# One gather in forty-six moved from GpSimd to row-by-row transfers issued by SyncE, in a three-layer graph network

## The chip, the cores and the metric

The kernel runs on one core of a Trainium2 chip. The metric is the device time of one execution in microseconds. Engines are called PE (TensorE), DVE (VectorE), ACT (ScalarE), POOL (GpSimd) and SP (SyncE); SP computes nothing here and only issues transfers, as POOL does with its gathers.

## The reference

6250 nodes with 256 features each, 100,000 edges sorted by destination, three edge types, three layers:

```
ew = edge_attr @ edge_w + edge_b                    # 100000 x 256, once
for l in range(3):
    msg = relu(x[src] * ew)                         # gather of 100000 rows
    out = x @ roots[l] + biases[l]
    for i in range(3):
        h = segment_sum(msg * (edge_type == i), dst) / max(count_i, 1)
        out = out + h @ weights[l, i]
    x = x + relu(out)
result = layernorm(x0 + x)
```

The 100,000 sources are random nodes, so `x[src]` is a fetch of 100,000 separate rows of 1 KB from the chip's main memory, in every layer.

## The kernel before, in words

Edges are cut into tiles of 128; two tiles are a pair, two pairs (four tiles) share one buffer `xs` of 128 partitions x 2 x 2 x 256 numbers. There are 391 pairs, 782 tiles a layer. A layer is one loop over steps `it`, written out by hand; each engine runs the instructions in the order in which the loop issues them. One step takes in one pair:

- `gather(pair(9))` (line 989, in `gather_pair`): POOL issues two indirect transfers, one a tile; each reads 128 indices of `src_io` from the chip's own memory and fetches 128 rows. There are `ROWS` = 8 buffers `xs`, so POOL may be up to eight buffers ahead of their readers.
- SP loads `at`, the edges' attributes of eight pairs (line 570, three buffers), for `pair(9)`; `make_ew` uses it at `pair(5)`, four steps later (line 624, PE, after ACT's seed on line 611).
- `weigh(pair(3))`: DVE multiplies (line 646) and ACT applies relu (line 648), over a whole buffer of two pairs. `one_hot` (line 654) makes 0/1 matrices from destinations, and `reduce(pair(0))` (lines 668 and 676, PE) sums messages by node with them. `add` (line 704, DVE) adds the sums into `acc` at a place held in registers, which line 697 loads eight at a time.
- A block of 128 nodes whose edges are done is multiplied by the weights (line 732), finished by DVE (lines 763 and 766) and, in layers 0 and 1, written by SP to the table `x_mid` (line 768) that the next layer gathers from. In the last layer SP loads `x0` (line 792) and stores the output (line 785) instead.

The first six pairs of a layer need nothing from node block 0 (it is added later) and are gathered before the layer begins. All other gathers of the layer wait until the whole of `x_mid` is written. Every transfer of SP and ACT is given one of eight completion semaphores in turn, and before a semaphore is used again the issuing engine waits until the transfer that used it before has landed.

Of the kernel before, what the change touches and what calls it, by code (L numbers as in the profile page):

```python
# [8 lines left out]
F32 = mybir.dt.float32  # L9
BF = mybir.dt.bfloat16  # L10
I32 = mybir.dt.int32
# [431 lines left out]
def ordered_path(ctx, tc, x, attr_laid, A, weights, roots, biases, edge_w, edge_b, out, src, src_i, seg, place_i, consts, x_root,  # L443
# [6 lines left out]
    nc = tc.nc  # L450
    P = 128
    N, D = x.shape
    E = src.shape[0]
# [4 lines left out]
    U = T // 2  # L458
# [4 lines left out]
    order, _, moved, least, most = schedule(N, E, 1)  # L463
# [16 lines left out]
    big = ctx.enter_context(tc.tile_pool(name="big", bufs=1))  # L480
# [51 lines left out]
    rows = ctx.enter_context(tc.tile_pool(name="rows", bufs=ROWS))  # L532
# [6 lines left out]
    def first_of(p, n):  # L539
        return p == 0 or order[p - 1] // n != order[p] // n  # L540

    def last_of(p, n):
        return p == U - 1 or order[p + 1] // n != order[p] // n

    def opens(u):
        p = order.index(u)
        return p == 0 or span_of[order[p - 1]] != span_of[u]
# [20 lines left out]
    def load_at(g):  # L568
        at = edge.tile([P, GROUP // 2, P], F32, name="at", bufs=3)
        nc.sync.dma_start(at.rearrange("p q e -> p (q e)"), attr_laid[g])  # L570
        return at
# [8 lines left out]
    def layer(l, r_sb, b_sb, ats, early, pools):  # L580
# [5 lines left out]
        x_rows = x if l == 0 else x_mid[l - 1]  # L586
        w_sb = wpool.tile([P, R * DC, D], F32, name="w_sb")
        CH = DC + 1 if l == 0 else DC
        xs, ew_ps, ohs, h_ps, h_ss, o_ps, rs = {}, {}, {}, {}, {}, {}, {}
        x0s, mvs, oh_bs, t_ss, places = {}, {}, {}, {}, []  # L590
        r_next, ats_next, early_next = (None, None), {}, {}
        seen = [0]

        def gather(u):
            p = order.index(u)
            if p < FIRST:
                xs[u // 2] = early[u // 2]
            else:
                if first_of(p, 2):
                    xs[u // 2] = room(rows, D)  # L600
                gather_pair(nc, xs[u // 2], x_rows, src_i, u)

        def pairs_of(q):
            return range(min(2, U - 2 * q))
# [23 lines left out]
        def gather_early(p):  # L628
            u = order[p]
            if first_of(p, 2):  # L630
                early_next[u // 2] = room(rows, D)
            gather_pair(nc, early_next[u // 2], x_mid[l], src_i, u)
# [172 lines left out]
        for it in range(-11, max(starts) + 7):  # L805
            def pair(k):
                return order[it + k] if 0 <= it + k < U else None
            if pair(AHEAD) is not None:
                gather(pair(AHEAD))
            if l < L - 1 and 0 <= it + AHEAD - U < FIRST:  # L810
                gather_early(it + AHEAD - U)
            if l == 0 and it == 20:
                find_came()
            if pair(AHEAD) is not None and pair(AHEAD) // GROUP not in ats:
                ats[pair(AHEAD) // GROUP] = load_at(pair(AHEAD) // GROUP)
            if l == 0 and it >= -4 and (it + 4) % 20 == 0 and (it + 4) // 20 * 6 < NT - 1:
                load_x((it + 4) // 20 * 6)
            if it == 10:
                nc.sync.dma_start(w_sb, weights[l].rearrange("r (c p) e -> p (r c) e", p=P))
            if l == L - 1 and it + 2 in root_at:  # L820
                load_x0(root_at[it + 2])
            if l < L - 1 and it == U - 10:
                r_next = load_root(l + 1)
            if l < L - 1 and U - 10 <= it < U - 8:
                ats_next[at_groups[it - U + 10]] = load_at(at_groups[it - U + 10])

            if pair(0) is not None:
                reduce(pair(0))
            if pair(-1) is not None and closes(pair(-1)) and turned(span_of[pair(-1)]):
                take(span_of[pair(-1)])  # L830
            if pair(5) is not None and first_of(it + 5, 2):
                make_ew(pair(5) // 2)
            for lag in (LAG + 1, LAG):
                if pair(-lag) is not None and closes(pair(-lag)) and turned(span_of[pair(-lag)]) == (lag > LAG):
                    add(span_of[pair(-lag)])
            if pair(-1) is not None and closes(pair(-1)) and turned(span_of[pair(-1)]):
                turn(span_of[pair(-1)])
            if pair(3) is not None and first_of(it + 3, 2):
                if l > 0 and it + 3 < FIRST:
                    complete(pair(3) // 2)  # L840
                if pair(3) // 2 != order[-1] // 2:
                    weigh(pair(3) // 2)

            if pair(3) is not None and pair(3) // 2 == order[-1] // 2:
                weigh(pair(3) // 2, range(pair(3) % 2, pair(3) % 2 + 1))
            if pair(6) is not None and first_of(it + 6, 2):
                seed_ew(pair(6) // 2)
            if it in root_at:
                root_turn(root_at[it])
            if it - 1 in root_at:  # L850
                root_turned(root_at[it - 1])
            if it - 2 in root_at:
                root_mul(root_at[it - 2])
            if it - 3 in root_at:
                root_keep(root_at[it - 3])
            if it == moved:
                move()
            if it - 2 == moved:
                clear(P)
            if it + 1 in node_at and slot_of(node_at[it + 1]) == 0:  # L860
                wrap()
            if it in node_at:
                node_mul(node_at[it], 0)
            if it - 1 in node_at:
                node_end(node_at[it - 1], 0)
            if it - 2 in node_at:
                node_mul(node_at[it - 2], 1)
            if it - 3 in node_at:
                node_end(node_at[it - 3], 1)
                clear(slot_of(node_at[it - 3]))  # L870
            if it - 4 in node_at and l == L - 1:
                deviate(node_at[it - 4])
            if it - 5 in node_at and l == L - 1:
                norm(node_at[it - 5])
            if pair(2) is not None and first_of(it + 2, 2):
                one_hot(pair(2) // 2)
# [21 lines left out]
FIRST = 6  # L898

ASTRAY = 1024  # L900


def spans_of(N, E):
# [31 lines left out]
def schedule(N, E, lag):  # L935

    P = 128
    U = -(-E // (2 * P))
    NT = -(-N // P)
    done = []
    for c in range(NT):
        edges = E * min(1.0, (P * (c + 1) / N) ** 0.5)
        done.append(U if c == NT - 1 else min(U, -(-int(edges) // (2 * P)) + 4))
    K = first_pairs(N, E)
    spans = spans_of(N, E)
    for c in range(NT):  # L950
        span = next(s for s in spans if s[1] >= done[c])
        done[c] = span[1] + turned(span)
    order = list(range(K, U)) + list(range(K - 1, -1, -1))
    moved = done[1] - K + lag
    starts = [0] * NT
    step = moved
    for c in range(2, NT):
        step = starts[c] = max(done[c] - K + lag + 1, step + 4)

    whole = U - int(0.55 * K)  # L960
    starts[1] = max(whole + lag, step + 4)
    starts[0] = max(U + lag - 1, starts[1] + 4)

    node = lambda e: int(N * min(1.0, max(0.0, e / E)) ** 2)
    least = [node(2 * P * u - ASTRAY) for u in range(U)]
    most = [node(2 * P * u + ASTRAY) for u in range(U)]


    for u, v in spans:
        p = max(order.index(u), order.index(v - 1)) + lag + turned((u, v))  # L970
        if u >= K:
            assert all(p <= starts[c] or least[u] >= P * (c + 1) for c in range(2, NT))
            assert p <= moved or least[u] >= 2 * P
            assert all(p < starts[c] or least[u] >= P * c for c in range(8, NT, 8))
            for b in range(RING // P + 1, (most[u] + WIN - 1) // P + 1):
                assert (moved + 2 if b - RING // P == 1 else starts[b - RING // P] + 3) < p
        else:
            assert most[u] <= 2 * P and (p <= starts[1] or most[u] + WIN <= P)
    return order, starts, moved, least, most


def room(rows, D):

    return rows.tile([128, 2, 2, D], F32, name="xs", bufs=ROWS)


def gather_pair(nc, xs, x_rows, src_i, u):
    for i in range(2):
        nc.gpsimd.indirect_dma_start(  # L989
            out=xs[:, u % 2, i, :], out_offset=None, in_=x_rows[:, :],  # L990
            in_offset=bass.IndirectOffsetOnAxis(ap=src_i[:, 2 * u + i:2 * u + i + 1], axis=0))
# [3 lines left out]
def kernel(ctx, tc, x, src, dst, edge_attr, edge_type, weights, roots, biases, edge_w,  # L995
# [32 lines left out]
    with tc.tile_pool(name="look", bufs=1) as look, tc.tile_pool(name="look_p", bufs=2, space=PSUM) as look_p, \  # L1028
# [7 lines left out]
        limits = look.tile([1, 2, U], F32, name="limits")  # L1036
        nc.gpsimd.iota(limits, pattern=[[2 * ASTRAY, 2], [2 * P, U]], base=-ASTRAY, channel_multiplier=0,
                       allow_small_or_imprecise_dtypes=True)
# [120 lines left out]
```

## Time and profile before

| | |
|---|---|
| time, median of 3 runs | 2981.86 us (2981.05 to 2984.7) |
| profiled execution: its time / its span | 2986.33 us / 2984.5 us |
| POOL busy | 2239.8 us in 2355 instructions |
| PE busy | 2656.7 us |
| DVE busy | 1935.5 us |
| ACT busy | 1561.9 us |
| mean granted TensorE clock | 0.97 |
| mean DMA rate | 130 GB/s |

A busy share says how much of the span an engine's instructions took, not whether it set the pace. [...] An operation that is marked "q", as in SPq, is the engine's queue: issuing transfers, loading registers, waiting for semaphores.

### The profile page before, as it was taken

The page shows a single profiled execution, that of the slowest core. Times are in us where ns is not written, and L with a number is a line of the kernel's source. Part 1 is how long each engine was busy: PE and PEld are TensorE (multiplying, and loading weights), DVE is VectorE, ACT ScalarE, POOL GpSimd, SP SyncE. Part 2 cuts the span into 40 slices and gives each one's busy share as a digit, 9 for nine tenths or more (in the row PEclk, how much of TensorE's full clock was granted, in tenths as well). Part 3 has the DMA queues.
Part 4 walks back from the last instruction along what each step waited for, and adds up shares of the span by engine and source line. Part 5 has one row for each costly group of instructions (what it writes and reads, how often), then busy time and mean ns, then how long its engine had stood idle before and what let it go on. Part 6 is the DMA issues. An engine that isn't in the chain of part 4 may idle for free.

```text
span 2984.5 us, 45518 instructions
## 1 busy us (share of the span) xinstructions
PE 2656.7 (89%) x13712; PEld 1836.6 (62%) x13712; DVE 1935.5 (65%) x5485; ACT 1561.9 (52%) x2487; POOL 2239.8 (75%) x2355
## 2 busy tenths in 40 slices
PE   5999999999998888998899889778899889889887
PEld 2666677776765555556676666455555666666655
DVE  6666677777764455566666676445566677777754
ACT  4666666666665445554444444435555544444453
POOL 7777777777777777777777777777777777777775
PEclk9999999999999999999999999899999999999998
DMA  5544444444444434444444444434444444444443
GB/s 163 149 144 136 143 128 128 129 126 130 128 135 127 122 112 125 122 120 128 128 128 125 130 131 133 127 113 143 132 137 133 134 133 136 131 129 131 128 124 95
DMA packets 173574, 387.52 MB, mean 130 GB/s; under 512 B 43450, under 2 KB 78924, under 8 KB 173324
## 3 DMA queue, kind: packets, MB, share of 16 engines
q0 software_dynamic: 112608, 307.65, 36.0%
q1 hardware_dynamic: 53136, 68.50, 7.3%
q10 hardware_dynamic: 7580, 8.37, 0.9%
q8 instruction: 117, 1.92, 0.3%
q14 instruction: 133, 1.09, 0.1%
HBM read 364.88 MB, written 19.46 MB: 129 GB/s over the span
## 4 chain that ended last, share of the span: by engine, by line
PE 40%; POOL 16%; DMA 15%; issue 13%; DVE 7%; ACT 6%; DVEq 1%; ACTq 0%; POOLq 0%
POOL xs L989 16%; DMA xs<-x_mid,src_io 12%; PE ew_p L624 11%; PE h_p L668 9%; PE h_p L676 7%; PE o_p L732 6%; PE r_p L717 4%; DVE xs L646 3%; DMA xs<-in_x_dram,src_io 3%; ACT ew_p L611 2%; ACT xs L648 2%; PE h_p L688 1%; DVE x_root L763 1%; DVE acc L704 1%; PE r_p L709 1%
## 5 line engine op out<-in xcount | busy, mean ns | idle before, releaser
L989 POOL DMA_INDIRECT xs<-x_mid,src_io x1564 | 1490.6, 953 | 485.5 <-issue 373.0
L648 ACT ACTIVATE xs<-xs 128x1024 f32<-128x1024 f32 (+1 forms) x588 | 617.8, 1051 | 1241.4 <-DVE xs L646 1233.3
L646 DVE TENSOR_TENSOR xs<-ew_p,xs 128x512 f32<-128x512 f32 x1167 | 777.2, 684 | 643.9 <-DMA xs<-x_mid,src_io 489.8
L989 POOL DMA_INDIRECT xs<-in_x_dram,src_io x770 | 734.4, 954 | 234.7 <-issue 185.9
L624 PE MATMUL ew_p<-ew_sb,at 64*128 64x512 f32 x2346 | 761.6, 657 | 108.4 <-ACT ew_p L611 102.6
L676 PEld LDWEIGHTS h_p<-oh,xs 128*128 128x128 f32 x5160 | 657.9, 197 | 233.9 <-DVE acc L704 106.3
L676 PE MATMUL h_p<-oh,xs 128*128 128x120 f32 x5160 | 717.0, 287 | 64.8 <-DVE acc L704 59.2
L611 ACT ACTIVATE ew_p<-seed 128x512 f32<-128x512 f32 x1161 | 639.9, 583 | 0.0
L668 PE MATMUL h_p<-xs,oh 128*120 128x256 f32 x2088 | 554.5, 397 | 24.1 <-DVE acc L704 24.0
L654 DVE TENSOR_SCALAR oh<-iota_w,seg_o 128x120 f32<-128x120 f32 x2346 | 517.1, 298 | 0.0
L732 PE MATMUL o_p<-w_sb,acc 128*128 128x256 f32 (+1 forms) x1716 | 445.4, 396 | 29.6 <-DVE x_root L763 14.9
L704 DVE TENSOR_TENSOR acc<-h_p,acc 128x240 f32 (+1 forms) x732 | 323.6, 442 | 180.7 <-PE o_p L732 42.4
L668 PEld LDWEIGHTS h_p<-xs,oh 128*120 128x120 f32 x2088 | 356.6, 187 | 123.3 <-DVE acc L704 34.4
L732 PEld LDWEIGHTS o_p<-w_sb,acc 128*128 128x128 f32 (+1 forms) x1716 | 310.9, 192 | 161.8 <-issue 38.5
L624 PEld LDWEIGHTS ew_p<-ew_sb,at 64*128 64x128 f32 x2346 | 230.0, 188 | 262.1 <-ACT ew_p L611 184.4
L763 DVE SCALAR_TENSOR_TENSOR x_root<-o_p,inv,x_root 128x256 f32<-128x256 f32 (+1 forms) x429 | 205.9, 480 | 59.1 <-PE o_p L732 51.7
L717 PE MATMUL r_p<-r_sb,t_s 128*128 128x256 f32 x588 | 171.4, 417 | 31.6 <-ACT t_s L713 31.6
L658 ACT ACTIVATE oh_b<-oh 128x480 bf16<-128x480 f32 x196 | 116.7, 596 | 102.2 <-DVE oh L654 101.6
L717 PEld LDWEIGHTS r_p<-r_sb,t_s 128*128 128x128 f32 x588 | 106.7, 202 | 83.5 <-ACT t_s L713 47.2
L749 ACT ACTIVATE acc<-zero_o 128x768 f32<-128x768 f32 (+1 forms) x150 | 140.1, 934 | 21.5 <-PE r_p L732 16.4
L688 PEld LDWEIGHTS h_p<-ident_o,h_s 120*128 120x128 f32 x342 | 35.7, 144 | 145.9 <-ACT h_s L684 81.9
L720 DVE TENSOR_TENSOR x_root<-r_p,b_sb 128x256 f32<-128x256 f32 x147 | 61.6, 419 | 64.4 <-PE r_p L717 38.8
(103 smaller groups left out, 898.8 us busy)
## 6 DMA issues: line engine op xcount, KB each, us to landing
at<-in_attr_laid_dram SPq DMA_DIRECT2D x147, 256.0 KB
xs<-x_mid,src_io POOLq DMA_INDIRECT x1564, 2.8
xs<-in_x_dram,src_io POOLq DMA_INDIRECT x770, 2.8
x_mid<-x_all SPq DMA_DIRECT2D x96, 128.0 KB
x_all<-in_x_dram ACTq DMA_DIRECT2D x8, 768.0 KB
x<-in_x_dram SPq DMA_DIRECT2D x48, 128.0 KB
out_dram<-x_all SPq DMA_DIRECT2D x48, 128.0 KB
w_sb<-in_L_gnn_weights_dram SPq DMA_DIRECT2D x3, 768.0 KB
```

What stands on the lines that cost most here:

```text
L611: nc.scalar.activation(ew_ps[u], seed, AF.Copy)
L624: nc.tensor.matmul(ew_ps[2 * q + k].rearrange("p i d -> p (i d)"), at[half, :], ew_sb[half].rearrange("p i d -> p (i d)"), start=False, st ...
L646: nc.vector.tensor_mul(xs[q][:, k], ew_ps[2 * q + k], xs[q][:, k])
L648: nc.scalar.activation(there, there, AF.Relu)
L654: nc.vector.tensor_scalar(ohs[q][:, t, :], iota_w, seg[:, 4 * q + t:4 * q + t + 1], None, op0=ALU.is_equal)
L668: nc.tensor.matmul(by_node[:WK, :D], ohs[u // 2][:, t, :], xs[u // 2][:, u % 2, i, :], start=(i == 0 and opens(u)), stop=(i == 1 and close ...
L676: nc.tensor.matmul(h_ps[span][:, d, :], xs[u // 2][:, u % 2, i, d * P:(d + 1) * P] if d < DC else full_ones, (ohs if d < DC else oh_bs)[u ...
L704: nc.vector.tensor_tensor(there, h_ps[span][:, :CH].rearrange("p c (r w) -> p c r w", r=R), there, op=ALU.add)
L717: nc.tensor.matmul(rs[c][:, 1, :], t_ss[c][:, d, :], r_sb[:, d, :], start=(d == 0), stop=(d == DC - 1))
L732: nc.tensor.matmul(o_p[:n, j, :], acc[:, d, r, slot:slot + n], w_sb[:, r * DC + d, :], start=(d == 0), stop=(d == DC - 1))
L763: nc.vector.scalar_tensor_tensor(root, o_p[:n, j, :], inv[:n, c, r:r + 1], root, op0=ALU.mult, op1=ALU.add)
L989: nc.gpsimd.indirect_dma_start(out=xs[:, u % 2, i, :], out_offset=None, in_=x_rows[:, :], in_offset=bass.IndirectOffsetOnAxis(ap=src_i[:, ...
```

## The change

In each layer 17 of the 782 tiles are no longer gathered by POOL. SP fetches their rows one by one: a list of the sources, `src_s`, lies in the chip's memory; for every eight rows SP loads eight of its numbers into registers, and each row is a transfer of its own, of 1 KB, whose source address comes from a register. The 128 rows of such a tile are issued six in a step (`SINGLES`), from step 0 on, at a place in the loop after `gather` and before the load of `at`, so 17 tiles take 363 steps of some 410. The tile is the second one of the second pair that is in its buffer, and its position lies at least six steps behind the step in which its last row is issued. `weigh`, which reads it, comes three steps before that position. These buffers are a kind of their own, `xs_s`, of which there are two; the other three tiles in them are gathered as before. The same 17 positions are used in all three layers: 28, 48, 70 and so on about every 21 steps up to 369.

```diff
+    per = -(-U * 2 // P)
+    src_s = big.tile([P, per * P], I32, name="src_s")
+    whole = E // (per * P)
+    nc.scalar.dma_start(src_s[:whole, :], src[:whole * per * P].rearrange("(a e) -> a e", e=per * P))
+    singles = []
+    for p in range(U - 12):
+        first = SINGLE_FROM + (len(singles) + 1) * P // SINGLES + 6
+        if p >= first and first_of(p, 2) and order[p] // 2 == order[p + 1] // 2 and order[p] < (whole * per) // 2 - 2:
+            singles.append((order[p + 1], 1))
+    single_of = {u // 2: (u, i) for u, i in singles}
...
-                if first_of(p, 2):
+                if first_of(p, 2) and u // 2 not in single_of:
                     xs[u // 2] = room(rows, D)
-                gather_pair(nc, xs[u // 2], x_rows, src_i, u)
+                gather_pair(nc, xs[u // 2], x_rows, src_i, u, [i for i in range(2) if (u, i) not in singles])
...
+        def fetch(n):
+
+            for r in range(n, n + SINGLES):
+                if r // P >= len(singles):
+                    return
+                u, i = singles[r // P]
+                if r % P == 0:
+                    xs[u // 2] = rows.tile([P, 2, 2, D], F32, name="xs_s", bufs=2)
+                t = 2 * u + i
+                if r % LOADED == 0:
+                    _, loaded = nc.values_load_multi_w_load_instructions(
+                        src_s[t // per:t // per + 1, t % per * P + r % P:t % per * P + r % P + LOADED],
+                        engines=[mybir.EngineType.SP], min_val=0, max_val=N - 1,
+                        skip_runtime_bounds_check_because="it is the number of a node")
+                    sources[:] = loaded
+                nc.sync.dma_start(xs[u // 2][r % P:r % P + 1, u % 2, i, :], x_rows[bass.ds(sources[r % LOADED], 1), :])
...
                 gather(pair(AHEAD))
             if l < L - 1 and 0 <= it + AHEAD - U < FIRST:
                 gather_early(it + AHEAD - U)
+            if it >= SINGLE_FROM:
+                fetch((it - SINGLE_FROM) * SINGLES)
...
+SINGLE_FROM = 0
+SINGLES = 6
+LOADED = 8
...
-def gather_pair(nc, xs, x_rows, src_i, u):
-    for i in range(2):
+def gather_pair(nc, xs, x_rows, src_i, u, tiles=range(2)):
+    for i in tiles:
```

In the built program SP's part of one row is two instructions: a register operation that turns the node's number into an address, and the transfer. Eight rows have one register load ahead of them. That is 6528 transfers, 6528 register operations and 816 register loads in the three layers, beside some 350 transfers that SP issued before.

More of the change, by code (lines that the diff above doesn't have):

```diff
@@ L592, in layer @@
         seen = [0]
+        sources = []
         def gather(u):
```

## The prediction

> **What bounds the kernel now.** I read the page first, then the waits by engine, then POOL's and SP's instructions in order of time. The page's chain of work that ended last, and its groups:
>
> ```profile
> PE 40%; POOL 16%; DMA 15%; issue 13%; DVE 7%; ACT 6%; DVEq 1%; ACTq 0%; POOLq 0%
> ...
> L989 POOL DMA_INDIRECT xs<-x_mid,src_io x1564 | 1490.6, 953 | 485.5 <-issue 373.0
> L646 DVE TENSOR_TENSOR xs<-ew_p,xs 128x512 f32<-128x512 f32 x1167 | 777.2, 684 | 643.9 <-DMA xs<-x_mid,src_io 489.8
> L989 POOL DMA_INDIRECT xs<-in_x_dram,src_io x770 | 734.4, 954 | 234.7 <-issue 185.9
> ```
>
> PE has the largest share of the chain, but POOL, DMA and issue together have 44%. DVE's multiplication waits mostly for gathers. Is POOL late, or the transfer slow? The waits of POOL, and the instructions of line 989:
>
> ```profile
> POOL xs L989 <- issue: 558.9, 1834, 0.3
> POOL xs L989 <- DMA x_mid<-x_all: 5.2, 1, 5.2
> ...
> L989 POOL DMA_INDIRECT xs<-x_mid,src_io x1564: 941/947/1376, 991.3 to 2966.2; - x196
> L989 POOL DMA_INDIRECT x_root<-in_x_dram,src_io x12: 942/948/1802, 5.6 to 20.1; - x12
> ...
>   DVE xs L646: 623.1, 415
> ...
> DMA to landing us min/median/max: 2.7/2.8/6.2
> ```
>
> The last two rows but one say who waited for the gathers; the last, how long a gather takes from issue to landing. POOL's idle time is 0.3 us ahead of each gather, waiting for nothing, and one wait of 5.2 us. It gathers without a pause from 5.6 to 2966.2 us: 2960.6 us for 2345 intervals, 1.26 us each. A step has two, so 2.52 us. In order of time at the layers' border:
>
> ```profile
> 1003.82 0.95 POOL L989 DMA_INDIRECT xs<-x_mid,src_io  x1 [0.31 <-issue]
> 1005.07 0.94 POOL L989 DMA_INDIRECT xs<-x_mid,src_io  x1 [0.30 <-issue]
> 1011.19 0.94 POOL L989 DMA_INDIRECT xs<-x_mid,src_io  x1 [5.18 <-DMA x_mid<-x_all]
> 1012.44 0.95 POOL L989 DMA_INDIRECT xs<-x_mid,src_io  x1 [0.30 <-issue]
> ```
>
> So POOL's issue of gathers is the pace of the kernel, although the page calls it 75% busy; PE stands close behind with 89%. SP, on the other hand, mostly stands in front of a semaphore:
>
> ```profile
> SPq L768 <- DVE x_all L766: 1190.4, 74, 40.6
> SPq L785 <- DVE x_all L783: 401.7, 27, 66.8
> SPq L768 <- DVE acc L704: 330.3, 21, 29.0
> ```
>
> **What the change takes away.** 17 gathers a layer, 51 in all, at 1.26 us: 64 us less on POOL. That is the most it can gain, and it needs every row of SP's to be there in time.
>
> **What it adds on SP: the price of one row.** The trace has no transfer of one row and none with its address in a register. The nearest rows are SP's transfers, a register load and the register operations behind it (minimum/median/maximum in ns):
>
> ```profile
> L768 SPq DMA_DIRECT2D x_mid<-x_all x98: 246/320/330, 145.4 to 1995.9; - x98
> L570 SPq DMA_DIRECT2D at<-in_attr_laid_dram x147: 327/383/1502, 35.3 to 2911.8; - x147
> L697 DVEq TENSOR_LOAD <-place_i x135: 593/597/1058, 59.4 to 2910.4; - x135
> L704 DVEq FUSED_REGOPS  x729: 69/69/69, 60.1 to 2911.1; - x183
> L1104 SPq TENSOR_LOAD <-flag x1: 462/462/462, 17.6 to 17.6; - x1
> L1104 SPq FUSED_REGOPS  x1: 186/186/186, 18.2 to 18.2; - x1
> ```
>
> and SP's transfers that follow one another:
>
> ```profile
> 314.69 0.33 SPq L768 DMA_DIRECT2D x_mid<-x_all  x1
> 315.11 0.38 SPq L570 DMA_DIRECT2D at<-in_attr_laid_dram  x1
> 35.27 1.28 SPq L570 DMA_DIRECT2D at<-in_attr_laid_dram  x3
> 36.59 0.46 SPq L819 DMA_DIRECT2D w_sb<-in_L_gnn_weights_dram  x1
> ```
>
> The issue takes SP about 0.3 us, little of it from the size: 128 KB of `x_mid` take 0.320 us, 256 KB of `at` 0.383. Three in a row take 1.28 us, 0.40 each without the gap of 0.04 (35.27 + 1.28 to 36.59). Terms of one row:
>
> - The transfer: at most 0.40 (back to back); the shortest seen is 0.246. One row is less than any of these, but has a register address and follows closely on another. I take 0.28. Nothing excludes a price under 0.246; I go down to 0.20.
> - The register operation: 0.07 (DVE's 69 ns, 729 times; the one on SP took 0.186).
> - Two gaps of 0.04: 0.08.
> - An eighth of a register load with its gap: (0.462 + 0.04)/8 = 0.06 to (0.597 + 0.04)/8 = 0.08. I take 0.07.
>
> Together 0.28 + 0.07 + 0.08 + 0.07 = 0.50 us. From below, 0.20 + 0.07 + 0.08 + 0.07 = 0.42; from above, 0.40 + 0.07 + 0.08 + 0.07 = 0.62.
>
> [...]
>
> **What SP has to do in a layer, and by when.** 17 x 128 = 2176 rows. Among them SP issues its other transfers, 94 in layers 0 and 1 (45 `at`, 48 `x_mid`, one of weights) and 142 in layer 2 (45 `at`, 49 `x0`, 47 stores, one of weights), counted in the built program; at 0.42 us each (314.69 to 315.11) that is 39 + 39 + 60 = 138 us.
>
> SP may begin in layers 1 and 2 when `x_mid` has landed, which is when POOL goes on at 1011.19 with pair 6. The last fetched tile is in pair 369; in the old pace POOL would have come to its end 364 pairs x 2.52 = 917 us later. In layer 0 SP is ready at about 37 us (the three loads of `at` above), and POOL, which began at 5.6, reaches the end of pair 369 after 370 x 2.52 = 932, at 938: 901 us. What a transfer needs to land is about the same on both sides. So SP has 901 + 2 x 917 = 2735 us for its 6528 rows and 138 us of other transfers, and it keeps the pace if a row costs no more than (2735 - 138)/6528 = 0.40 us; for the whole gain of 21 us a layer, 0.39.
>
> At 0.50 it needs 3264 + 138 = 3402 us, 667 too many. Behind SP's late rows wait DVE's multiplication of the tile, and with it ACT, PE and the node blocks; and in SP's own queue, behind `fetch`, the load of `at`, for which PE has only four steps, and the writes of `x_mid`. So no engine can run past it: what SP is late, the layer is late. The semaphore waits of SP in the list above (1190.4 us and the others) are no reserve: they are SP running ahead to the next `x_mid` write, and shrink to nothing as SP falls behind.
>
> Behind the last row, 22 pairs of the layer and the six early ones are left. POOL has by then filled its buffers, so these 28 steps go by PE's pace. With PE 89% busy a step can shrink by 0.28 us at most, 8 us a layer; I take 5, 15 in all.
>
> Costed at nothing: the six thousand reads of 1 KB (6.7 MB beside the 387.52 MB that the page gives); the one load of `src_s`, behind ACT's first work; DVE's wait for eight more semaphores 51 times; the two more buffers. If their cover is gone, the largest is the reads: they run beside the gathers.
>
> Sum against the profiled execution's own 2986.33 us: + 667 - 15 = 3638. The median of the runs is 4.5 us below that execution, so **3634 us**.
>
> **The rivals.**
>
> *SP keeps up, and the kernel is faster.* This decides at 0.40 us a row, a transfer of 0.18: SP would then never be late, and POOL's 51 gathers fall out of the pace. Then the time is 2986 - 64 - 4.5 = 2918 us, or up to some 30 us more if PE's own waits come in between. For it: the transfers shown are all of 106 or more rows of 1 or 2 KB, and the shortest took 0.246; a single row could be far cheaper. Against it: 128 KB and 256 KB differ by 0.06 only, so most of the price is for the instruction. [...] I give it 0.11.
>
> *No difference.* A row of 0.39 to 0.40, gain and lateness cancelling: 0.03.
>
> *The completion semaphores.* Each row waits until the transfer eight before it has landed. With a landing of 2.8 us that allows a row every 0.35 us and does not bind; it decides from 8 x 0.50 = 4.0 us of landing. At the longest landing shown, 6.2 us, a row would take 0.78, and the time is 2982 + 6528 x 0.78 + 138 - 2735 - 15 = 5460 us. Speaking for it: an `at` of 256 KB takes its place in the round, too. Against it: a row is 1 KB. I give it 0.06 as the main cause.
>
> *SP late*, as forecast: 0.80.
>
> **How the numbers follow.** The forecast is the likeliest case. The range is that of the row's price: 0.42 gives 2742 + 138 - 2735 - 15 = 130 more, 3112; 0.62 gives 4047 + 138 - 2735 - 15 = 1435 more, 4417. I put the ends at 3100 and 4420; left out are SP keeping up and no difference (0.14) and the worst of the semaphores. A measurement of this kernel can tell about 0.2% (6 us) from no change. Slower by more than that: 0.80 + 0.06 = 0.86; within: 0.03; faster: 0.11.
>
> **What would show it.** Right: `L630` transfers on SPq of 0.2 to 0.4 us with hardly a pause between them through most of each layer; DVE's line for the multiplication waiting on `xs_s` from SP, or PE on `at`; POOL's gaps no longer 0.3 us but waits for buffers (PE or ACT); SP's waits for DVE near zero; the other 2295 gathers still 0.95 us each. Wrong: POOL still at 1.26 us per gather without a pause and SP waiting for DVE again, which is the faster rival; SP's rows each waiting for a transfer of SP's, which is the rival of the semaphores. A row's price off from 0.50 by 0.01 moves the time by 65 us, so that term is where the forecast is weakest.

## The result, and the profile after

The change takes 3859.97 us (median of 4 runs, 3858.43 to 3862.67) against 2981.95 us: a ratio of 1.294, 95% interval 1.2924 to 1.2956. The profiled execution of after took 3860.1 us, its span is 3858.3 us. The forecast was 3634, its range 3100 to 4420, on the side of slower.

The chain of work that ended last, and the group that now idles longest for a transfer, from the page of after:

```profile
SPq 45%; PE 25%; issue 17%; DMA 8%; DVE 4%; ACT 1%; DVEq 0%; POOL 0%; ACTq 0%; POOLq 0%
...
L653 PE MATMUL ew_p<-ew_sb,at 64*128 64x512 f32 x2346 | 813.5, 754 | 979.4 <-DMA at<-in_attr_laid_dram 952.1
```

POOL had 16% of the chain and has none; SP's queue, which was not in it, has 45%. (Line numbers are those of each run's own kernel: the write of `x_mid`, line 768 before, is 797 in after and 792 in e6_fixed_again.) What the engines see of it is PE waiting 952 us for `at`, which stands behind the rows in SP's queue; DVE waits for `xs_s` itself only 147 us (92.0 and 55.2 us). SP's own waits in after, and what its rows and register loads took (ns, minimum/median/maximum):

```profile
SPq L630 <- DMA x_all<-in_x_dram: 43.3, 8, 9.0
SPq L797 <- DMA xs<-x_mid,src_io: 40.7, 7, 19.5
SPq L814 <- DVE x_all L812: 40.4, 1, 40.4
...
SPq L797 <- DVE x_all L795: 6.1, 3, 4.4
...
SPq L630 <- DMA xs_s<-in_x_dram: 1.5, 1, 1.5
```

```profile
L630 SPq FUSED_REGOPS  x6528: 37/37/48, 46.6 to 3809.7; - x198
L630 SPq MOVE xs_s<-in_x_dram x2176: 29/29/38, 46.6 to 1294.0; - x198
L630 SPq DMA_DIRECT2D xs_s<-in_x_dram x2176: 224/228/312, 46.7 to 1294.1; - x198
...
L625 SPq TENSOR_LOAD <-src_s x816: 567/794/1309, 45.9 to 3805.6; - x164
```

The wait for DVE ahead of the `x_mid` writes was 1190.4 us and is 6.1: SP has no time left to wait. The waits for earlier rows to land come to 1.5 us. POOL, whose longest wait before was 5.2 us, now waits for ACT, and its gathers still take 0.95 us each:

```profile
POOL xs L1023 <- ACT ew_p L640: 219.1, 76, 12.1
POOL xs L1023 <- ACT xs L677: 183.5, 45, 16.1
```

How the rows follow one another stands in the chain in order of time (start, us; line 630 is a row's transfer, 625 a register load):

```profile
618.12 0.27 SPq L630
618.57 0.23 SPq L630
618.98 0.23 SPq L630
619.39 0.23 SPq L630
619.80 0.23 SPq L630
620.22 0.23 SPq L630
620.63 0.23 SPq L630
621.04 0.23 SPq L630
621.31 0.79 SPq L625
622.28 0.27 SPq L630
```

A row every 0.41 us, and eight rows with one load from 618.12 to 622.28, 4.16 us: 0.52 us a row. So it goes on through each layer, with only SP's other transfers in between. SP's first and last row stand at 46.7 and 1294.1 us in layer 0, at 1340.4 and 2542.8 in layer 1, at 2585.8 and 3809.8 in layer 2: 3674 us of the 3858. At the layers' borders, where no rows are issued, the work runs fast; the border between layers 0 and 1, before and after (columns: window, length, busy time of PE, of weight loads, DVE, ACT and POOL, granted clock, DMA share, GB/s):

```profile
938.00:1011.00 73.00, 57.99 (x343) 40.73 (x339) 31.42 (x87) 32.52 (x49) 51.56 (x55) 0.96 0.40 115
```

```profile
1294.00:1340.00 46.00, 45.14 (x319) 32.90 (x317) 25.67 (x73) 27.64 (x42) 29.19 (x31) 1.00 0.43 127
```

After, PE is busy 45.14 of 46 us and is the pace there; before, it was busy 57.99 of 73 us, which is 79%. The window after holds somewhat less work, 319 matmuls against 343.

### The profile page after: what moved, and what is told of

It reads as the page before. It is cut to its first block, busy times and chain, and to the rows that moved or that the text cites. A ratio compares the mean times of both kernels' runs of the same rounds, so it can differ in the third digit from the quotient of the medians.

```text
span 3858.3 us, 66689 instructions
## 1 busy us (share of the span) xinstructions
PE 2808.6 (73%) x13712; PEld 1933.9 (50%) x13712; DVE 1923.0 (50%) x5485; ACT 1572.2 (41%) x2487; POOL 2192.9 (57%) x2304
## 3 DMA queue, kind: packets, MB, share of 16 engines
q1 hardware_dynamic: 66192, 75.21, 6.4%
## 4 chain that ended last, share of the span: by engine, by line
SPq 45%; PE 25%; issue 17%; DMA 8%; DVE 4%; ACT 1%; DVEq 0%; POOL 0%; ACTq 0%; POOLq 0%
SPq L630 32%; SPq L625 11%; PE ew_p L653 8%; PE h_p L705 6%; DMA at<-in_attr_laid_dram 6%; PE h_p L697 4%; PE o_p L761 4%; PE r_p L746 1%; DVE xs L675 1%; DMA x_all<-in_x_dram 1%; DVE oh L683 1%; DVE x_root L792 1%; DVE acc L733 1%; PE h_p L717 1%; SPq L581 1%
## 5 line engine op out<-in xcount | busy, mean ns | idle before, releaser
L1023 POOL DMA_INDIRECT xs<-x_mid,src_io x1428 | 1363.4, 955 | 1024.7 <-issue 684.1
L653 PE MATMUL ew_p<-ew_sb,at 64*128 64x512 f32 x2346 | 813.5, 754 | 979.4 <-DMA at<-in_attr_laid_dram 952.1
L677 ACT ACTIVATE xs<-xs 128x1024 f32<-128x1024 f32 x537 | 563.2, 1049 | 1122.5 <-DVE xs L675 1046.4
L1023 POOL DMA_INDIRECT xs<-in_x_dram,src_io x702 | 668.9, 953 | 562.5 <-issue 370.9
L675 DVE TENSOR_TENSOR xs<-ew_p,xs 128x512 f32<-128x512 f32 x1065 | 681.5, 680 | 231.0 <-PE ew_p L653 230.8
L705 PE MATMUL h_p<-oh,xs 128*128 128x120 f32 x4728 | 671.1, 292 | 12.9 <-DVE acc L733 12.4
L761 PE MATMUL o_p<-w_sb,acc 128*128 128x256 f32 (+1 forms) x1716 | 480.2, 420 | 11.9 <-DVE x_root L792 6.3
L742 ACT ACTIVATE t_s<-r_p 128x256 f32<-128x256 f32 x147 | 54.7, 372 | 340.5 <-PE r_p L738 340.4
L677 ACT ACTIVATE xs_s<-xs_s 128x1024 f32<-128x1024 f32 x51 | 53.9, 1057 | 287.5 <-DVE xs_s L675 217.2
L675 DVE TENSOR_TENSOR xs_s<-ew_p,xs_s 128x512 f32<-128x512 f32 x102 | 68.6, 685 | 170.5 <-DMA xs_s<-x_mid 92.0
```

The lines of the kernel that those rows point to most:

```text
L653: nc.tensor.matmul(ew_ps[2 * q + k].rearrange("p i d -> p (i d)"), at[half, :], ew_sb[half].rearrange("p i d -> p (i d)"), start=False, st ...
L675: nc.vector.tensor_mul(xs[q][:, k], ew_ps[2 * q + k], xs[q][:, k])
L677: nc.scalar.activation(there, there, AF.Relu)
L705: nc.tensor.matmul(h_ps[span][:, d, :], xs[u // 2][:, u % 2, i, d * P:(d + 1) * P] if d < DC else full_ones, (ohs if d < DC else oh_bs)[u ...
L761: nc.tensor.matmul(o_p[:n, j, :], acc[:, d, r, slot:slot + n], w_sb[:, r * DC + d, :], start=(d == 0), stop=(d == DC - 1))
L1023: nc.gpsimd.indirect_dma_start(out=xs[:, u % 2, i, :], out_offset=None, in_=x_rows[:, :], in_offset=bass.IndirectOffsetOnAxis(ap=src_i[:, ...
```

## The experiments

The chips of these runs need 3628 to 3675 us for the kernel before, where the chip of the prediction needed 2982; every run is therefore compared with runs of the kernel before on its own chip. On these chips SP's trace has pauses between and within instructions, of 0.7 us as the expectation of e5_four_again has them, 1207 in e1_four: in the change's run here the register operation takes up to 1396 ns (48 at most in after), a row's transfer up to 1397 (312) and a semaphore instruction of the rows' line up to 712 (281). They are not all that differs. On these chips DVE and ACT also have waits for which the profile names no releaser (`remote`), even in e4_plain, where SP issues few transfers; the traces of before and after have none. What makes the pauses and these waits stays open, and no run had a chip like the first.

```profile
L630 SPq FUSED_REGOPS  x6528: 1/37/1396, 48.3 to 4932.7; - x198
```

```profile
DVE acc L728 <- remote: 330.3, 80, 12.9
ACT h_s L708 <- remote: 150.4, 41, 11.1
```

The first line is from the change's run here, the other two are from e4_plain. Ratios with an interval, and those of the runs with four rows, are from 4 to 6 executions; e2_five, the three runs with fixed sources, e9_load32 and e7_at_act were executed once each.

| run | what | time, us | kernel before, us | ratio |
|---|---|---|---|---|
| e8_change_here | the change, six rows a step, 51 tiles | 4991 | 3628 | 1.376 [1.370, 1.381] |
| e2_five | five rows, 42 tiles | 4626 | 3668 | 1.261 |
| e1_four, e5_four_again, e11_four_third | four rows, 33 tiles | 4081, 4082, 4008 | 3668, 3675, 3628 | 1.114, 1.109, 1.105 |
| e10_three | three rows, 24 tiles | 3786 | 3628 | 1.043 [1.040, 1.047] |
| e3_fixed, e6_fixed_again, e12_fixed_third | six rows, sources fixed | 3836, 3831, 3795 | 3668, 3675, 3628 | 1.046, 1.042, 1.046 |
| e4_plain | one plain transfer a tile | 3706 | 3668 | 1.012 [1.008, 1.016] |
| e9_load32 | the change, 32 sources a load | 4852 | 3628 | 1.337 |
| e7_at_act | the change, `at` issued by ACT | 5282 | 3675 | 1.437 |

**Is it SP's instructions or the rows' transfers?** The register work of each row is taken away, the transfer stays:

```diff
-                if r % LOADED == 0:
-                    _, loaded = ...
-                    sources[:] = loaded
-                nc.sync.dma_start(xs[u // 2][r % P:r % P + 1, u % 2, i, :], x_rows[bass.ds(sources[r % LOADED], 1), :])
+                row = (37 * r) % N
+                nc.sync.dma_start(xs[u // 2][r % P:r % P + 1, u % 2, i, :], x_rows[row:row + 1, :])
```

> Six rows in a step as in the change, but each row's source is a fixed row that is written into the instruction, not a register: no register load, no register operation. It leaves out the right sources of the 51 tiles. The rows, their bytes, their landings and their semaphores stay. Theory: a row costs SP 0.23 + 0.04 = 0.27 us, six 1.6 and the other transfers 0.2, 1.8 us a step, under 2.52: SP keeps up and the time is that of 51 gathers less, about 2920 us. Rival (landing, semaphores, DMA load): nothing of it has changed, so about 3860 us or, with rows issued faster, no less.

> Six rows in a step from fixed rows, without register loads and register operations, again. It leaves out the right sources of the 51 tiles. Theory: 0.27 us a row, 1.8 us a step, SP keeps up, about 2920 us. Rival (landing, semaphores, DMA load of 6528 rows): about 3860 us.

> Six rows in a step from fixed rows, without register loads and register operations, once more; it leaves out the right sources of the 51 tiles. On a chip that takes 2982 us for the kernel before, theory: 0.30 us a row (the pace between pauses in the earlier run), 2.0 us a step with the other transfers, SP keeps up, about 2920 us. Rival (landing, semaphores, DMA load): about 3860 us. On a chip that takes some 3650 us: 1.04 as before.

The same 6528 transfers, landings and semaphores cost 4.2% to 4.6%, where the change costs 37.6%. So on these chips nearly all of the loss comes of the sources in registers, of the loads and register instructions that SP runs for them, and not of the rows on the DMA engines. Where the 4.2% to 4.6% come from stays open. SP's rows and waits in e6_fixed_again:

```profile
L625 SPq DMA_DIRECT2D xs_s<-x_mid x4352: 2/250/1463, 1323.3 to 3767.2; - x198
```

```profile
SPq L792 <- DVE x_all L790: 319.3, 61, 13.7
SPq L809 <- DVE x_all L807: 134.1, 17, 48.3
```

SP waits for DVE again ahead of the writes, some 453 us in all, so it isn't late there. The time foretold for a chip of 2982 us, 2920, could not be seen on these.

**Does it keep up with fewer rows?** Five, four and three in a step:

```diff
-SINGLES = 6
+SINGLES = 5   # and 4, and 3
```

> Five rows in a step: 14 tiles a layer, 42 in all, 5376 rows. Theory: SP needs 5 x 0.52 + 0.2 = 2.8 us a step, over 2.52, so SP is the pace still, and the row stretches take 5376 x 0.52 + 285 = 3080 us, with the 184 us outside them about 3265 us, a ratio of 1.095. Rival (loss in proportion to the rows): 2982 + 878 x 42/51 = 3705 us.

> Four rows in a step instead of six: 11 tiles a layer, 33 in all, 4224 rows. Theory (the pace is the time SP takes to issue a row, 0.52 us with its share of the register load): SP needs 4 x 0.52 and about 0.2 for its other transfers, 2.3 us a step, under GpSimd's 2.52, so SP keeps up and 33 gathers of 1.26 us fall away: about 2940 us, a ratio of 0.986, with SP waiting for DVE again and GpSimd at 1.25 us a gather without a pause. Rival (the rows themselves do harm, by their landing, their completion semaphores or their load on the DMA engines): the loss shrinks with the number of rows, 878 x 33/51, about 3550 us.

> Four rows in a step again, because the chip of the first four runs needed 3668 us for the kernel before, where the chip of the prediction needed 2982; the traces of those runs show pauses of 0.7 us between SP's instructions (1207 in the run with four rows) that the trace of the change does not have. Theory, if the kernel before takes about 2982 us here: SP needs 2.3 us a step, under 2.52, keeps up, and the time is about 2940 us, a ratio of 0.986. Rival (loss in proportion to the rows): about 3550 us.

> Four rows in a step, once more, for a chip that takes 2982 us for the kernel before, if there is one. There, theory: 2.3 us of SP a step against 2.52, SP keeps up, 33 gathers of 1.26 us less: about 2940 us, a ratio of 0.986. Rival (loss in proportion to the rows): about 3550 us. On a chip that takes some 3650 us: 1.11 as before.

> Three rows in a step: 8 tiles a layer, 24 in all, 3072 rows. Theory: SP needs 3 x 0.78 + 0.3 = 2.6 us a step on these chips, where the kernel before takes 3.1, so SP keeps up; GpSimd is not the pace there (it waits for buffers in the run with one plain transfer a tile), so its 24 gathers gain nothing: 3670 to 3740 us, a ratio of 1.00 to 1.02. Where the kernel before takes 2982: 24 gathers of 1.26 us less, about 2952 us, 0.990. Rival (loss in proportion to the rows, by the ratio 1.11 of four rows): 1.08.

The loss is about 158 us with 24 tiles, 380 to 413 with 33, 958 with 42, 1363 with 51: 7, 12, 23 and 27 us a tile. A loss in proportion to the rows is out; it grows steeply between three and five rows, as it would where a queue comes to its limit. But no run is faster than before. Three rows were foretold at 1.00 to 1.02 and came out at 1.043; five were foretold at 1.095, with the price of a row on the first chip, and came out at 1.261. The 0.986 foretold for four rows on a chip like the first can't be judged here. With four rows (e1_four) PE already waits for `at`, with three (e10_three) hardly, and there SP still waits for DVE, some 294 us of 3767:

```profile
PE ew_p L653 <- DMA at<-in_attr_laid_dram: 521.0, 85, 21.7
```

```profile
SPq L797 <- DVE x_all L795: 210.2, 50, 42.2
SPq L814 <- DVE x_all L812: 83.8, 8, 65.2
```

```profile
PE ew_p L653 <- DMA at<-in_attr_laid_dram: 24.9, 6, 9.6
```

**GpSimd's side alone.** One plain transfer of 128 neighbouring rows in place of 128 rows (the lines that it replaces are left out):

```diff
...
+                if r % P == P - 1:
+                    nc.sync.dma_start(xs[u // 2][:, u % 2, i, :], x_rows[:P, :])
```

> Each of the 51 tiles is fetched by one plain transfer of 128 neighbouring rows, issued where the last of the row transfers stood. It leaves out the right sources of the 51 tiles. It is GpSimd's side of the change alone. Theory: 51 gathers at 1.26 us less, about 2918 us, a ratio of 0.979, and GpSimd still without a pause. Rival (PE or ACT takes over as the pace before the whole 64 us are gained): 2930 to 2955 us, with waits for buffers ahead of GpSimd's gathers.

A miss: 51 gathers less, with 51 plain transfers in their place, made it 1.2% slower, not 2.1% faster, and why it is slower stays open. POOL is not the pace on this chip; it waits for ACT, and idles long where the profile names nothing that it waits for (`issue`):

```profile
POOL xs L1018 <- issue: 1014.1, 1861, 15.1
POOL xs L1018 <- ACT ew_p L635: 135.7, 77, 11.0
POOL xs L1018 <- ACT h_s L708: 73.2, 30, 3.7
```

Those idle times are up to 15.1 us long. Before, on the first chip, none of them was over 0.3; in after, where POOL waits for others too, the longest is 14.8. So this run says nothing of the 64 us on the first chip; they were not tested.

**Is it the place of `at` in the queue?** In `load_at`:

```diff
-        nc.sync.dma_start(at.rearrange("p q e -> p (q e)"), attr_laid[g])
+        nc.scalar.dma_start(at.rearrange("p q e -> p (q e)"), attr_laid[g])
```

> The change with the load of at issued by ACT, so that it no longer stands behind the rows in SP's queue; PE's waits for it (952 us in the trace of the change) can go. Theory: the rows remain the pace, because DVE needs them for its tiles; SP only saves its 147 loads of at, at some 0.4 to 0.75 us: 3750 to 3800 us, with the waits now at DVE for xs_s. Rival (the loss comes of the load of at, held up behind the rows): at most some 3100 us.

> The change itself, as a reference for the runs of this study, since their chips needed some 3670 us for the kernel before and not 2982. Theory: SP's issue of rows is the pace here too. In the run with at on ACT its rows took 5059 us, 0.775 each with the pauses of 0.7 us that SP makes on these chips; with the loads of at back on SP and the 220 us outside: about 5400 us, a ratio of 1.47. If the chip needs 2982 us for the kernel before, 3860 us and 1.294 again. Rival (the price does not hang on SP's instructions): 3670 + 878 = 4550 us.

The change here was foretold at about 5400 us, 1.47, from the run with `at` on ACT, and took 4991. Waits of the change here, and then of the run with `at` on ACT:

```profile
PE ew_p L653 <- DMA at<-in_attr_laid_dram: 1610.2, 128, 24.7
...
DVE xs_s L675 <- DMA xs_s<-x_mid: 106.3, 18, 19.0
```

```profile
DVE xs_s L675 <- DMA xs_s<-x_mid: 878.2, 31, 51.6
...
DVE xs_s L675 <- DMA xs_s<-in_x_dram: 543.0, 17, 51.9
```

PE's 1610 us for `at` become DVE's 1421 us for the rows, and nothing is gained (1.437 against 1.376, on two chips; why it is even slower stays open). The expectation was right on where the waits go; the small gain that it foretold did not show. `at` is only where the lateness is met first; the rows are its cause.

**The register load.** Thirty-two sources at a time:

```diff
-LOADED = 8
+LOADED = 32
```

> The change with 32 sources in one register load instead of 8: 204 loads instead of 816, everything else alike. Theory: a load takes SP some 0.9 us beyond the rows, on these chips up to 1.2, so 612 loads less are 550 to 730 us off the time of the change on the same chip: about 4750 us (3310 where the change takes 3860). If a load's price is by the register and not by the load: no difference. Rival (the pace is not SP's issue): no difference.

The time falls by 139 us, not by 550 to 730. The loads in the change here and in this run:

```profile
L625 SPq TENSOR_LOAD <-src_s x816: 2/786/1734, 47.7 to 4928.6; - x164
```

```profile
L625 SPq TENSOR_LOAD <-src_s x204: 645/2142/2600, 45.7 to 4772.0; - x102
```

Eight registers take 0.786 us, 32 take 2.142: (2.142 - 0.786)/24 = 0.057 us a register and 0.33 a load. Most of the price goes by the register, so 612 loads less save 612 x 0.33 = 202 us at most. The expectation had the price by the load.

## Why the prediction was right

**What bounds the kernel, and that SP cannot be passed:** borne out by the profile after. SP issues nearly without a break through each layer, its waits for DVE ahead of the `x_mid` writes are gone, POOL has left the chain, and `at` and `xs_s` are what others wait for. On their chips, e6 and e8 show that the register work makes most of the difference, and e7 that moving `at` out of the queue does not help.

**The price of a row** was 0.50 and is 0.52, by errors that cancel; that it came so near is luck. The transfer took 0.228 us instead of 0.28, less than the shortest one of the trace before (0.246); the register operation 0.037 instead of 0.07; but there is a third instruction, which the account of the change does not have, a MOVE of 0.029, and with it three gaps of some 0.04 (0.412 - 0.228 - 0.037 - 0.029 = 0.118); and a load of eight registers adds 4.16 - 8 x 0.412 = 0.86 us, 0.108 a row instead of 0.07.

**The sum.** The forecast was 222 us too low (3638 against 3860 for the profiled executions). By its terms:

- rows: 6528 x 0.52 = 3395 instead of 3264, 131 more;
- all else in the stretches of rows, SP's other transfers above all: 3674 - 3395 = 279 us instead of 138, 141 more. For 43 us of it rows wait for the loads of `x_all`, 768 KB each, that ACT issued;
- outside the stretches of rows: 3858 - 3674 = 184 us. The forecast had 2984.5 - 2735 - 15 = 234, so the part that runs faster once POOL's buffers are full was under-sized by 50. It took PE as 89% busy in every step, where at the border it was 79%; the 28 steps there took 46 us with PE full, where before they took 73.

131 + 141 - 50 = 222. So here, too, one error hides a part of the others.

**The rivals.** SP keeping up: out, by the ratio and the trace; the transfer takes 0.228 us, not the 0.18 it needed, and it isn't alone: 6528 starts of 1 KB, with their register work 0.52 us each, are the pace. No difference: out, by the ratio. The completion semaphores: they are there, as 43 us behind `x_all` and 1.5 us behind rows, and not the cause.

**Not shown:** the gain of 64 us, since no run had a chip on which POOL is the pace and SP keeps up. By the trace of after, four rows would need 4 x 0.52 + 0.26 (279 us over 1089 steps) = 2.3 us of SP in a step of 2.52, an estimate; whether that brings the 42 us of its 33 gathers is open.

## What to carry to other kernels

An engine that only issues transfers has a rate, too, here 0.52 us a row, of which the transfer took 0.228: add up all that it does for one item (address, moves, gaps, its share of the register load, not the transfer alone) and set it against the pace of the step that it is to keep. Its long waits for others are no proof of room in each step; they show slack for the old work (1190.4 us for DVE ahead of the `x_mid` writes before, 6.1 after). When a queue comes late, look for the wait at whatever stands behind it, here `at` (952 us of PE); moving that away moved the wait, not the time (1610 us of PE, then 1421 of DVE; ratios 1.376 and 1.437).

## What the runs showed of the hardware that was not expected

- A transfer of one row uses little of the DMA system: the 6528 rows added 66192 - 53136 = 13056 packets to their queue, two each, and the queue's packets took 6.4% of the 16 engines' span after, 7.3% before. What they cost in after is issue, 0.52 us of SP each.
- The granted TensorE clock fell from 0.97 to 0.85 over the span while PE waited more, and was 1.00 in the border window in which PE was busy 45.14 of 46 us; the mean matmul took 410 ns instead of 382.
- A load of eight numbers into SP's registers took 0.79 us, one of 32 took 2.14: most of the price goes by the register.
- The same kernel before took 2982 us on one chip and 3628 to 3675 on others. No trace of it was taken there; in the traces of the other runs there, gathers take the same 0.95 us, SP has pauses (register operations of up to 1396 ns, 48 in after), and DVE and ACT have waits without a releaser in the profile (330.3 and 150.4 us in e4_plain).
